# Gram products in three separate groups, their chain a period later, and layer 3's coefficients a quarter sooner

## The chip, the cores and the metric

The kernel runs on one core of a Trainium2 chip. The metric is the device time of one execution in microseconds (us), the median over several runs. One execution was also taken by the hardware profiler; all busy times, waits and timelines below come from it.

## What is computed

The input x has 16 images of 64 channels with 128 by 128 points, float32. Four layers follow, each of the form x = x + f(gn(x)), where gn is a group normalization over pairs of channels.

```
x = x + conv_w · (gram(gn(x)) · gn(x))      # layer 0: gram = gn(x) gn(x)^T / N, per image
x = x + |kx * gn(x)| + |ky * gn(x)|         # layer 1: two fixed 3x3 filters
x = x + conv3x3(shift(gn(x)), W) + b        # layer 2: some channels shifted by one column
x = x + clip(leaky(batchnorm(conv1x1(conv3x3(gn(x), w_bin)))), 0, 255)   # layer 3
```

Layer 0 needs the 64 by 64 matrix of channel products (the Gram matrix) of a whole image before the first point of that image can be made. From it the kernel works out one 64 by 64 mixing matrix for each image, with the normalization folded in, and the coefficients of layer 1's normalization. Layer 3's batch normalization is over all images, so the output is made in a last pass.

## The kernel before

An image is cut into 8 row blocks (`NS`), and the main loop runs over steps of four quarters, q0 to q3. In step s each stage works on the block `s - start - 8 b` of image b: `Front` (layers 0 and 1) starts at 15, `Layer2` at 25, `Layer3` at 35. So a period of 8 steps is one image for every stage, and three images are in work at once. Each engine gets its instructions in the order in which the loops write them down (`InOrder`), and nothing is reordered afterwards: an instruction that waits holds everything behind it on its engine.

In a step TensorE makes layer 3's products in q0 and q1 (first into `one`, with weights `w`, then into `two`), the mixing products `po` in q1, and layer 2's in q2 and q3 (`one` and `two`, with weights `wi`). There is one buffer `one` only. ScalarE (ACT) copies it out with the bias: `c<-one,b_sb` at the start of q1 for layer 3, and `c<-one,co` at the start of q3 for layer 2. The next product into `one` can't start before that copy is done. ACT also normalizes (`v`, `xh`), takes absolute values (`u`, `e`), squares for the statistics (`junk`), copies layer 3's half of the differences (`qd<-d`), and takes the square roots of the coefficient chains (`sd<-nv`). VectorE (DVE) makes layer 1's filter sums (`u`, `e`), the differences `d`, adds `x` and `y`, and does nearly all of the small arithmetic. GpSimd (POOL) scales edge columns and starts the DMAs of layer 2's copies `qd<-d`. SyncE (SP) starts the loads and stores.

The Gram products of the images from 7 on (class `Gram`) are made far ahead of their use. In eight steps the image's rows are loaded in 8 pieces of 512 KB (`xr`, three buffers) and copied by ACT into `xw`, one piece at a time (`rows_to_columns`). Then come 128 products of 65 columns in three parts of 44, 42 and 42 (`part`), which add up in one region of the PSUM bank `bank`. The same bank holds the results of all small products. Then `gram_chain` starts: a generator that alternates small products on TensorE with small arithmetic on DVE, a piece for each call of `tick()`, which comes at the end of each quarter. From the copy `gs` to the last `co` it runs through 17 quarters.

`coefficients` is a shorter chain of four quarters: a reduction of the sums, a product, a square root, and the coefficients. Layer 3's starts in q1 of the step in which layer 2 has finished the image (`i == NS`), after the last block's squares. `Layer3.prepare(0)` uses them one step later in q1; there DVE also makes `edge_lower` and `edge_upper` first.

For the period that is looked at below, steps 84 to 91: the Gram parts are those of image 12 (q0 and q2 of step 85, q0 of step 86); the chain of image 12 runs from q2 of step 86 to q2 of step 90; the copies into `xw` are those of image 13; layer 3's coefficients are those of image 7 (q1 of step 89 to q0 of step 90).

Of the kernel before, what the change touches and what calls it, by code (L numbers as in the profile page):

```python
# [10 lines left out]
F32 = mybir.dt.float32  # L11
# [97 lines left out]
def tile_kernel(ctx: ExitStack, tc: tile.TileContext, x, cw_h, w2_t, b2, wbin_t, w1_t, b1, gamma, beta, consts, out):  # L109
# [141 lines left out]
                    )  # L251


    chains = []

    def tick():
# [45 lines left out]

    def gram_chain(b, pg):

        gs = stp.tile([P, C + 1], F32, tag="gs", name=f"gs_{b}", bufs=1)
        dve.tensor_copy(gs, pg)
        if b > 1:
            yield
        gd = sm(C + 1)
        small_product(gd, k("same"), gs)  # L310
        yield
        g = stp.tile([P, C + 1], F32, tag="g", name=f"g_{b}", bufs=1)
        dve.tensor_scalar_mul(g, gd, 1.0 / HW)
        mu = g[:, C:C + 1]
        st = sv("st0", 2)
        dve.tensor_copy(st[:, 0:1], mu)

        junk0 = stp.tile([P, C], F32, tag="junk0", name=f"junk0_{b}", bufs=1)
        dve.scalar_tensor_tensor(
            junk0, g[:, 0:C], GN_EPS, k("Id"), op0=ALU.add, op1=ALU.mult, accum_out=st[:, 1:2]  # L320
        )
        if b > 1:
            yield
        pm = sm(2)
        small_product(pm, k("gavg"), st)
        yield
        r, me = sv("r"), sv("me", 2)
        yield from rstd(pm, r, me)

        vv = sv("vv", 3)  # L330
        dve.tensor_copy(vv[:, 0:1], mu)
        dve.tensor_sub(vv[:, 1:2], mu, me[:, 0:1])
        dve.tensor_scalar_mul(vv[:, 2:3], me[:, 0:1], -1.0)
        dd = stp.tile([P, 2, C], F32, tag="dd", name=f"dd_{b}", bufs=1)
        for s in range(2):
            dve.tensor_scalar_mul(dd[:, s, :], k("Id"), vv[:, s:s + 1])
        if b > 1:
            yield

        pr = sm(2 * C)  # L340
        small_product(pr, k("all"), dd.rearrange("p s c -> p (s c)"))
        yield

        t0 = stp.tile([P, C], F32, tag="t0", name=f"t0_{b}", bufs=1)
        dve.scalar_tensor_tensor(t0, pr[:, 0:C], vv[:, 0:1], g[:, 0:C], op0=ALU.mult, op1=ALU.subtract)
        cs = stp.tile([P, 2, C], F32, tag="cs", name=f"cs_{b}", bufs=1)
        for s in range(2):
            dve.scalar_tensor_tensor(cs[:, s, :], pr[:, C:2 * C], vv[:, 1:2], t0, op0=ALU.mult, op1=ALU.subtract)
        rc = stp.tile([P, C], F32, tag="rc", name=f"rc_{b}", bufs=1)
        dve.tensor_scalar(rc, cwh, r, 0.5, op0=ALU.mult, op1=ALU.mult)  # L350
        csf = cs.rearrange("p s c -> p (s c)")
        if b > 1:
            yield
        pq = sm(C)
        small_product(pq, csf, rc)
        yield
        r2 = sv("r2")
        dve.tensor_mul(r2, r, r)
        for s in range(2):
            rows = slice(s * C, (s + 1) * C)  # L360
            dve.tensor_scalar_mul(wbd[rows, rows], pq[rows], r2[rows])
        ad = stp.tile([P, C], F32, tag="ad", name=f"ad_{b}", bufs=1)
        dve.scalar_tensor_tensor(ad, pq, r2, k("Id"), op0=ALU.mult, op1=ALU.add)
        abd = stp.tile([P, P], F32, tag="abd", name=f"abd_{b}", bufs=EARLY + 3)
        dve.tensor_add(abd, wbd, k("I"))
        if b > 1:
            yield
        pd = sm(C + 3)
        small_product(pd[:, 0:C], csf, ad)
        small_product(pd[:, C:C + 2], abd, vv[:, 0:2])  # L370
        small_product(pd[:, C + 2:C + 3], wbd, vv[:, 2:3])
        yield
        pp = stp.tile([P, 2, C], F32, tag="pp", name=f"pp_{b}", bufs=1)
        dve.tensor_mul(
            pp, pd[:, 0:C].unsqueeze(1).to_broadcast([P, 2, C]), ad.unsqueeze(1).to_broadcast([P, 2, C])
        )
        av = sv("av", 3)
        dve.tensor_copy(av, pd[:, C:C + 3])
        if b > 1:
            yield  # L380
        pk = sm(1)
        small_product(pk, pp.rearrange("p s c -> p (s c)"), k("q"))
        if b > 1:
            yield
        bias = av[:, 2:3]
        st1 = sv("st1", 2)
        dve.tensor_add(st1[:, 0:1], av[:, 0:1], bias)
        t = sv("t1")
        dve.scalar_tensor_tensor(t, av[:, 1:2], av[:, 1:2], pk, op0=ALU.mult, op1=ALU.subtract)
        dve.scalar_tensor_tensor(  # L390
            st1[:, 1:2], st1[:, 0:1], st1[:, 0:1], t, op0=ALU.mult, op1=ALU.subtract
        )
        if b > 1:
            yield
        pm = sm(2)
        small_product(pm, k("gavg"), st1)
        yield

        co = stp.tile([P, 5], F32, tag="co1", name=f"co1_{b}", bufs=EARLY + 3)
        r, mean = co[:, 0:1], co[:, 3:4]  # L400
        yield from rstd(pm, r, co[:, 3:5], GN_EPS)
        dve.scalar_tensor_tensor(co[:, 1:2], bias, mean, r, op0=ALU.subtract, op1=ALU.mult)
        dve.reciprocal(co[:, 2:3], r)
        lead[b] = abd, co

    def gram_product(pg, w):

        s = w % 2
        pe.matmul(
            pg[s * C:(s + 1) * C, :], xw[:, w // 2, 0:C, s], xw[:, w // 2, :, s],  # L410
            start=(w < 2), stop=(w >= W - 2),
        )
        last[0] = s

# [8 lines left out]
    def first_gram():  # L423
# [13 lines left out]
        for m in range(NS + 1):  # L437
# [5 lines left out]
                    copy(xw[:, m * R:(m + 1) * R, 0:C, h], two[:, :, h * C:(h + 1) * C])  # L443
            if m > 0:
                for w in range(2 * R * (m - 1), 2 * R * m):
                    gram_product(pg, w)
        run(Front, 0, Front.first, 0)
        live[Front, 0].load(1)

# [6 lines left out]
                rows_to_columns(1, link - 2, rows[link - 2])  # L456

    class Gram:
        first, last = 0, NS + 1

        def __init__(self, b):
            self.b, self.xr, self.w = b, {}, 0

        def at(self, i, q):
            b = self.b
            if i < NS:
                if q == 0 and i != 1:
                    for m in range(i + (1 if i == 2 else 2) if i else 0, min(i + 3, NS)):
                        self.load(m)

                if q == 3 and i > 0:
                    for m in (0, 1) if i == 1 else (i,):
                        rows_to_columns(b, m, self.xr.pop(m))
                return
            n = 4 * (i - NS) + q

            self.part({0: 44, 2: 42, 4: 42}.get(n, 0))
            if n == 6:
                chains.append(gram_chain(b, self.pg))

        def part(self, n):
            if self.w == 0 and n:
                if self.b <= 2 * EARLY:
                    self.pg = ps_g.tile([P, CP, W], F32, tag="g", name=f"pg_{self.b}")[:, 0, 0:C + 1]
                else:

                    self.pg = bank[:, 3 * P:3 * P + C + 1]
            for _ in range(n // 2):
                for s in (1 - last[0], last[0]):
                    gram_product(self.pg, self.w + s)  # L490
                self.w += 2

        def load(self, m):
# [242 lines left out]
    class Layer2:  # L736
# [42 lines left out]
        def twin(self, n):  # L779
# [5 lines left out]
                flat(q[cols(1 - i), n])[:, 1:CP * (W + 2)], flat(d[cols(i), n])[:, 0:CP * (W + 2) - 1]  # L785
            )

        def square(self, i):
            act.activation(
                junk, tiles3[self.b][i].rearrange("p s j w -> p (s j w)"), AF.Square,  # L790
# [3 lines left out]
        def at(self, i, q):  # L794
            b = self.b
            closing = i + 1 == NS
            m = CP - 1 if closing else CP
            if q == 0:
                if 1 <= i:
                    two = self.p.pop(i - 1)[0]  # L800

# [13 lines left out]
            if q == 1:  # L815
# [25 lines left out]
                    pool.tensor_scalar_mul(t[:, :, W - 1], t[:, :, W - 1], k("keep1"))  # L841
                if i + 2 < NS:
                    self.load(i + 2)
                if i == NS:
                    self.square(i - 1)
                    chains.append(coefficients(self.st, lambda co: coefs3.update({b: co})))
            if q == 2:
                if 0 <= i < NS:
                    t = self.v[i]
# [26 lines left out]
            if q == "first of 3" and 0 <= i < NS:  # L876
                self.c = ring.tile([P, CP * W], F32, tag="c2", name=f"c2_{b}_{i}", bufs=1)
                act.activation(self.c, flat(self.p[i][1]), AF.Identity, bias=self.co[:, 5:6])
            if q == "last of 3" and -1 <= i < NS - 1:
                difference("d2", 1, self.v[i + 1], CP if i + 2 < NS else CP - 1)  # L880
                self.twin(1)
# [2 lines left out]
    class Layer3:  # L884
# [5 lines left out]
        def prepare(self, i):  # L890
# [5 lines left out]
                act.activation(dst, src, AF.Identity, bias=co[:, 1:2], scale=co[:, 0:1])  # L896

            if i == 0:
                self.co = coefs3.pop(b)

                self.edge = {}
                for half in ("lower", "upper"):
                    self.edge[half] = sv(f"edge_{half}", 2)
                    dve.tensor_scalar_mul(self.edge[half], self.co, k(half))
                norm(t[:, 0, :], tiles[NS - 1][:, 1, CP - 1, :], self.edge["lower"])
            else:
                norm(t[:, 0, :], tiles[i - 1][:, 1, CP - 1, :], self.co)
# [112 lines left out]
            fetched[0] += 1  # L1020

    for step in range(starts[2][1] - 2, steps):
        for q in range(4):
            for b in range(B):

# [5 lines left out]
            for stage, at in starts:  # L1031
                if stage is Front and q in (1, 3):
                    issue_rest()
                for b in range(B):
                    run(stage, b, step - at - NS * b, q)
            if q == 3:
                for b in range(B):
                    run(Layer2, b, step - starts[1][1] - NS * b, "last of 3")
            for b in range(1, B):
                at, n = pace[b]  # L1040
                if n == 1:
# [113 lines left out]
```

## Time and profile before

| | us |
|---|---|
| median of 3 runs | 2779.61 (2778.61 to 2780.83) |
| the profiled execution | 2778.27 |
| its span, first to last instruction | 2776.5 |
| TensorE busy | 2175.3 (78%) |
| DVE busy | 2192.0 (79%) |
| ACT busy | 2112.6 (76%) |
| POOL busy | 893.2 (32%) |

The span lacks 1.8 us that lie around the instructions. The shares are averages over a start of some 300 us, the main loop to about 2120 us, layer 3's last steps on TensorE to about 2320 us, and the last pass, which moves data only. In the lines of the profile each group is named by what it writes and reads, as in `two<-d,w`. The helper that keeps the order makes nearly every instruction carry the same source line, so the names and the engine tell them apart. A product in float32 leaves two records.

### The profile page before, as it was taken

Reading aid. Unit: us, or ns where it says so; the run is one execution under the profiler, and the core shown is the slowest. Engines: PE = TensorE matmul, PEld = TensorE weight load, DVE = VectorE, ACT = ScalarE, POOL = GpSimd, SP = SyncE. Lnnn points to the kernel's source line nnn. Section 1 sums busy time; section 2 is a strip of 40 time slices with the busy share of each in tenths; the row PEclk is TensorE's granted clock in tenths of the full one; section 3 lists DMA queues with packets and bytes.
Section 4 is the critical chain, followed back from the end, with each engine's and each line's share of the span. In section 5 each row is a group of like instructions: output and inputs, shape, how many; then the busy total and the mean of one; then the engine's idle time right before and its main releaser. Section 6 shows DMA issues by size and latency. Waiting matters only on the chain. (4 is left out here: it accounts for less than half of the span.)

```text
span 2776.5 us, 46105 instructions
## 1 busy us (share of the span) xinstructions
PE 2175.3 (78%) x14804; PEld 886.4 (32%) x14804; DVE 2192.0 (79%) x3623; ACT 2112.6 (76%) x3177; POOL 893.2 (32%) x1350
## 2 busy tenths in 40 slices
PE   6578899999999999999999999999999994000000
PEld 4233433434343434343433342333334641000000
DVE  4999999898989898989899999999996435333332
ACT  4766889898989898989898988999997667333332
POOL 2055434343434343434343344444444300000000
PEclk8689999999999999999999999999999997555555
DMA  8799888988888888888888777878877768999999
GB/s 205 201 229 238 211 216 226 231 215 229 218 227 213 229 221 221 216 230 216 230 218 227 206 188 197 217 202 219 215 199 195 213 196 288 420 420 420 420 420 384
DMA packets 693601, 685.96 MB, mean 247 GB/s; under 512 B 60096, under 2 KB 580448, under 8 KB 693360
## 3 DMA queue, kind: packets, MB, share of 16 engines
q1 hardware_dynamic: 668208, 613.83, 75.2%
q0 software_dynamic: 25152, 69.18, 10.2%
q8 instruction: 119, 1.95, 0.3%
q14 instruction: 122, 1.00, 0.1%
HBM read 346.23 MB, written 268.44 MB: 221 GB/s over the span
## 5 line engine op out<-in xcount | busy, mean ns | idle before, releaser
L73 PE MATMUL two<-d,w 128*64 128x508 f32 (+2 forms) x2560 | 846.8, 588 | 0.0
L73 PE MATMUL two<-d,wi 128*64 128x508 f32 (+3 forms) x1536 | 578.0, 579 | 0.0
L73 POOL DMA_DIRECT2D qd<-d x512 | 270.8, 531 | 903.7 <-DVE d L73 287.4
L73 PE MATMUL two<-qd,pk 128*64 128x512 f32 (+1 forms) x1024 | 519.0, 588 | 13.3 <-DMA qd<-d 12.5
L73 POOL TENSOR_SCALAR edges<-v,co 64x8 f32<-64x8 f32 x512 | 359.9, 703 | 307.7 <-ACT v L73 231.4
L73 DVE TENSOR_TENSOR d<-v 128x512 f32<-128x512 f32 (+1 forms) x512 | 345.6, 678 | 87.6 <-issue 55.5
L73 PE MATMUL one<-v,w 128*64 128x508 f32 (+2 forms) x1600 | 378.6, 599 | 34.8 <-ACT c L73 34.8
L73 PEld LDWEIGHTS two<-d,w 128*64 128x64 f32 x2560 | 263.1, 136 | 314.9 <-issue 278.5
L73 PE MATMUL one<-v,wi 128*64 128x508 f32 (+3 forms) x1536 | 358.5, 599 | 3.1 <-issue 2.6
L73 ACT COPY qd<-d 64x512 f32<-64x512 f32 x512 | 315.4, 616 | 20.8 <-DVE d L73 14.5
L73 DVE SCALAR_TENSOR_TENSOR e<-e 128x1032 f32<-128x1032 f32 (+1 forms) x256 | 312.9, 1222 | 0.0
L73 ACT ACTIVATE xh<-po,co 128x128 f32<-128x128 f32 (+1 forms) x480 | 275.2, 621 | 31.4 <-PE po L73 22.7
L73 POOL TENSOR_SCALAR v<-v,kc 128x9 f32<-128x9 f32 x256 | 234.6, 930 | 12.0
L73 DVE SCALAR_TENSOR_TENSOR y<-two,c 128x1024 f32<-128x1024 f32 x128 | 155.9, 1218 | 102.8 <-ACT v L73 65.4
L73 PEld LDWEIGHTS two<-d,wi 128*64 128x64 f32 x1536 | 175.6, 136 | 186.0 <-issue 169.6
L73 ACT ACTIVATE v<-x,co 128x512 f32<-128x512 f32 (+2 forms) x368 | 234.9, 705 | 0.0
L73 ACT ACTIVATE u<-u 128x1024 f32<-128x1024 f32 x128 | 135.3, 1057 | 106.8 <-DVE u L73 106.4
L73 PE MATMUL po<-x,abd 64*64 64x512 f32 (+1 forms) x1024 | 178.5, 643 | 44.0 <-ACT xh L73 41.0
L73 PEld LDWEIGHTS one<-v,w 128*64 128x64 f32 x1600 | 126.0, 139 | 237.9 <-issue 162.7
L73 PEld LDWEIGHTS two<-qd,pk 128*64 128x64 f32 x1024 | 136.3, 136 | 153.9 <-issue 110.6
L73 PEld LDWEIGHTS one<-v,wi 128*64 128x64 f32 x1536 | 108.9, 138 | 224.1 <-issue 209.0
L73 DVE SCALAR_TENSOR_TENSOR u<-xh 128x1170 f32<-128x1170 f32 x128 | 175.6, 1371 | 5.1 <-ACT xh L73 4.2
(165 smaller groups left out, 3333.9 us busy)
## 6 DMA issues: line engine op xcount, KB each, us to landing
x<-in_x SPq DMA_DIRECT2D x256, 256.0 KB, 4.1
x_d<-u SPq DMA_DIRECT2D x512, 128.0 KB, 3.8
y_d<-y SPq DMA_DIRECT2D x512, 128.0 KB, 4.0
x_d<-x SPq DMA_DIRECT2D x496, 128.0 KB, 2.6
xr<-in_x SPq DMA_DIRECT2D x120, 512.0 KB, 6.4
qd<-d POOLq DMA_DIRECT2D x256, 130.0 KB, 3.1
qd<-d POOLq DMA_DIRECT2D x256, 129.8 KB, 3.9
v<-x_d SPq DMA_DIRECT2D x448, 72.1 KB, 3.3
```

The costliest lines, as they stand in the source:

```text
L73: return self.tc.keep_in_program_order(call(*args, **kwargs))
```

## The change

Four things are changed, for the images from 7 on in the first three.

- The three parts of the Gram products stand in q1 of three successive steps (85, 86 and 87 in the period above) and are three groups, each started and closed by itself in a region of its own (`first`, `end`, `at`). `gram_chain` begins with a reduction over the three regions in place of a copy.
- The chain makes that reduction in q2 of step 87, and then waits until step `8 b - 4` before it goes on. So the chain of image 11 runs from q0 of step 84 to q3 of step 87, between the Gram parts of image 12. The buffer `gs` is doubled.
- Loads and copies of the row pieces are laid out anew: copies in q3 of step 87, q1 and q3 of 88, q3 of 89, q1 and q3 of 90, q3 of 91 and of 92; three loads in q0 of step 87, and each later one right behind a copy.
- For all images, layer 3's coefficient chain begins one quarter earlier, in q0, with the last block's squares at the end of that quarter, and the two `edge` vectors are made at its end instead of in `prepare`.

```
+    now = [0]
...
     def gram_chain(b, pg):
-        gs = stp.tile([P, C + 1], F32, tag="gs", name=f"gs_{b}", bufs=1)
-        dve.tensor_copy(gs, pg)
+        gs = stp.tile([P, C + 1], F32, tag="gs", name=f"gs_{b}", bufs=2)
+        if b > 2 * EARLY:
+            dve.tensor_reduce(gs, pg.rearrange("p (j c) -> p c j", j=3), axis=AX.X, op=ALU.add)
+        else:
+            dve.tensor_copy(gs, pg)
         if b > 1:
             yield
+        while b > 2 * EARLY and now[0] < NS * b - 4:
+            yield
...
-    def gram_product(pg, w):
+    def gram_product(pg, w, first, end):
...
-            start=(w < 2), stop=(w >= W - 2),
+            start=(w < first + 2), stop=(w >= end - 2),
...
     class Gram:
-        first, last = 0, NS + 1
+        first, last = 2, NS + 2
...
-            if i < NS:
-                if q == 0 and i != 1:
-                    for m in range(i + (1 if i == 2 else 2) if i else 0, min(i + 3, NS)):
-                        self.load(m)
-                if q == 3 and i > 0:
-                    for m in (0, 1) if i == 1 else (i,):
-                        rows_to_columns(b, m, self.xr.pop(m))
-                return
-            n = 4 * (i - NS) + q
-            self.part({0: 44, 2: 42, 4: 42}.get(n, 0))
-            if n == 6:
-                chains.append(gram_chain(b, self.pg))
+            n = 4 * (i - NS) + q
+            self.part({1: 44, 5: 42, 9: 42}.get(n, 0))
+            if n == 10:
+                chains.append(gram_chain(b, self.pg))
+            if i == 2 and q == 0:
+                for m in range(3):
+                    self.load(m)
+            m = {11: 0, 13: 1, 15: 2, 19: 3, 21: 4, 23: 5, 27: 6, 31: 7}.get(4 * i + q)
+            if m is not None:
+                rows_to_columns(b, m, self.xr.pop(m))
+                if m + 3 < NS:
+                    self.load(m + 3)
...
-                    self.pg = bank[:, 3 * P:3 * P + C + 1]
+                self.pg = bank[:, 2 * P:2 * P + 3 * (C + 1)]
+                first, end, at = self.w, self.w + n, self.parts * (C + 1)
+                self.parts += 1
             for _ in range(n // 2):
                 for s in (1 - last[0], last[0]):
-                    gram_product(self.pg, self.w + s)
+                    gram_product(self.pg[:, at:at + C + 1], self.w + s, first, end)
...
     class Layer2:
+        def done(self, co):
+            edge = {}
+            for half in ("lower", "upper"):
+                edge[half] = sv(f"edge_{half}", 2)
+                dve.tensor_scalar_mul(edge[half], co, k(half))
+            coefs3[self.b] = co, edge
...
             if q == 0:
+                if i == NS:
+                    chains.append(coefficients(self.st, self.done))
...
-                if i == NS:
-                    self.square(i - 1)
-                    chains.append(coefficients(self.st, lambda co: coefs3.update({b: co})))
...
+            if q == "last of 0" and i == NS:
+                self.square(i - 1)
...
     class Layer3:
             if i == 0:
-                self.co = coefs3.pop(b)
-                self.edge = {}
-                for half in ("lower", "upper"):
-                    self.edge[half] = sv(f"edge_{half}", 2)
-                    dve.tensor_scalar_mul(self.edge[half], self.co, k(half))
+                self.co, self.edge = coefs3.pop(b)
...
     for step in range(starts[2][1] - 2, steps):
+        now[0] = step
...
-            if q == 3:
+            if q in (0, 3):
                 for b in range(B):
-                    run(Layer2, b, step - starts[1][1] - NS * b, "last of 3")
+                    run(Layer2, b, step - starts[1][1] - NS * b, f"last of {q}")
```

More of the change, by code (lines that the diff above doesn't have):

```diff
@@ L445, in first_gram @@
                 for w in range(2 * R * (m - 1), 2 * R * m):
-                    gram_product(pg, w)
+                    gram_product(pg, w, 0, W)
         run(Front, 0, Front.first, 0)
@@ L458, in tile_kernel, with part @@
     class Gram:
-        first, last = 0, NS + 1
+        first, last = 2, NS + 2
         def __init__(self, b):
-            self.b, self.xr, self.w = b, {}, 0
+            self.b, self.xr, self.w, self.parts = b, {}, 0, 0
         def at(self, i, q):
             b = self.b
-            if i < NS:
-                if q == 0 and i != 1:
-                    for m in range(i + (1 if i == 2 else 2) if i else 0, min(i + 3, NS)):
-                        self.load(m)
-                if q == 3 and i > 0:
-                    for m in (0, 1) if i == 1 else (i,):
-                        rows_to_columns(b, m, self.xr.pop(m))
-                return
-            n = 4 * (i - NS) + q
-            self.part({0: 44, 2: 42, 4: 42}.get(n, 0))
-            if n == 6:
-                chains.append(gram_chain(b, self.pg))
-        def part(self, n):
-            if self.w == 0 and n:
-                if self.b <= 2 * EARLY:
+            n = 4 * (i - NS) + q
[10 more added lines that the diff above has]
+                    self.load(m + 3)
+        def part(self, n):
+            if not n:
+                return
+            first, end, at = 0, W, 0
+            if self.b <= 2 * EARLY:
+                if self.w == 0:
                     self.pg = ps_g.tile([P, CP, W], F32, tag="g", name=f"pg_{self.b}")[:, 0, 0:C + 1]
-                else:
-                    self.pg = bank[:, 3 * P:3 * P + C + 1]
+            else:
+                self.pg = bank[:, 2 * P:2 * P + 3 * (C + 1)]
+                first, end, at = self.w, self.w + n, self.parts * (C + 1)
+                self.parts += 1
             for _ in range(n // 2):
                 for s in (1 - last[0], last[0]):
-                    gram_product(self.pg, self.w + s)
+                    gram_product(self.pg[:, at:at + C + 1], self.w + s, first, end)
                 self.w += 2
```

## The prediction

> **What bounds the kernel now.** I read the slices of the page first, then the busy time of each engine in the windows of one period of eight steps, then the timelines around the one place where TensorE is idle.
>
> ```profile
> PE   6578899999999999999999999999999994000000
> DVE  4999999898989898989899999999996435333332
> ACT  4766889898989898989898988999997667333332
> ```
>
> From slice 5 to slice 32 all three engines are near full. An average can't say which one sets the pace, so I cut out the period in which image 12's Gram products are made, steps 84 to 91; each window goes from one start of layer 3's copy `c<-one,b_sb` (q1) to the next. Columns: stretch, length, busy time of PE, PEld, DVE, ACT, POOL, granted clock, DMA.
>
> ```profile
> 1158.00:1172.60 14.60, 14.60 (x90) 5.03 (x88) 14.23 (x20) 14.50 (x24) 7.17 (x10) 1.00 0.79 207
> 1172.60:1191.00 18.40, 18.40 (x230) 9.32 (x227) 13.76 (x18) 14.86 (x27) 5.00 (x10) 1.00 0.94 235
> 1191.00:1210.10 19.10, 19.10 (x170) 7.91 (x168) 16.15 (x29) 16.40 (x24) 5.42 (x10) 1.00 0.75 190
> 1210.10:1226.10 16.00, 16.00 (x90) 5.31 (x88) 15.55 (x40) 15.38 (x27) 5.94 (x10) 1.00 1.06 257
> 1226.10:1242.90 16.80, 16.80 (x134) 9.34 (x132) 16.40 (x29) 15.06 (x25) 6.06 (x10) 1.00 0.91 244
> 1242.90:1260.50 17.60, 16.80 (x95) 5.51 (x91) 17.29 (x31) 15.57 (x27) 8.06 (x10) 1.00 0.84 231
> 1260.50:1279.70 19.20, 15.04 (x66) 4.51 (x66) 18.55 (x39) 15.29 (x27) 5.98 (x11) 0.91 0.81 222
> 1279.70:1294.60 14.90, 14.90 (x74) 4.68 (x72) 14.53 (x20) 14.80 (x24) 7.41 (x11) 1.00 0.75 182
> ```
>
> TensorE is busy for the whole of six windows: it is the bound, and only the windows of steps 89 and 90 leave it idle, 0.80 + 4.16 us. There DVE is the fullest. DVE has time to spare in steps 85 and 86, where all three Gram parts stand (18.4 - 13.8 and 19.1 - 16.2 us), and none from 87 to 90, where the chain's vector work stands. The same period without Gram work (steps 116 to 123) takes 122.7 us, TensorE busy 122.0. Now the idle place, TensorE first, then ACT:
>
> ```profile
> 1265.80 1.03 PE L73 MATMUL two<-d,wi 128*64 128x508 f32 x4
> 1268.42 0.61 PE L73 MATMUL two<-qd,pk 128*64 128x512 f32 x1 [1.59 <-DMA qd<-d]
> ...
> 1272.92 4.48 PE L73 MATMUL one<-v,w 128*64 128x512 f32 x12 [2.57 <-ACT c L73]
> ```
>
> ```profile
> 1260.50 0.69 ACT L73 ACTIVATE c<-one,b_sb 128x512 f32<-128x512 f32 x1
> 1262.94 0.49 ACT L73 ACTIVATE v<-x,edge_lower 128x128 f32<-128x128 f32 x1 [1.75 <-DVE edge_lower L73]
> ...
> 1268.14 0.20 ACT L73 ACTIVATE sd<-nv 128x1 f32<-128x1 f32 x1 [2.05 <-DVE nv L73]
> ```
>
> TensorE waits 2.57 us for ACT to copy `one` out. ACT is late because it sat 1.75 us waiting for layer 3's coefficients and 2.05 us for the chain's last square root. After this idle time the twelve products take 4.48 us where they take 2.73 us elsewhere (at 1289.5): the clock is at half. So a period with Gram work loses 0.80 + 4.16 + (4.48 - 2.73) = **6.7 us**. Both late inputs are what the change moves.
>
> [...] 4.48 against 2.73 us after 1.59 + 2.57 us of idle time; a wait of 0.70 us in step 89 has no such tail. [...] In the changed order each Gram part waits for a DVE read of `bank`: part 2 for `ad`, made in q0 of its own step.
>
> **Part by part, for one period.** *Gram parts.* 256 product records before and after; the 88 of one part take 2.94 us, of the others 2.78. Moving them is worth nothing in itself: TensorE's total stays. But part 3 goes from step 86 to 87, which holds TensorE back 2.8 us just ahead of the steps where DVE and ACT are short.
>
> *Chain.* Its vector work is 0.47 + 0.36 + 1.2 + 0.86 + 1.28 + 0.27 + 0.45 + 0.71 + 1.04 = 6.6 us on DVE (from `g` at 1209.5 to `co` at 1272.2, less what stands between). It leaves 87 to 90 and goes to 84 to 87, where its last 2.2 us stay. Steps 84 to 86 take some 4.5 us more, within the 7.6 us spare in 85 and 86. Up to q0 of step 90 DVE is freed of 2.7 us. The reduction of three parts in place of a copy: 0.22 us for 65 elements, about 1 ns more an element (`pp`, 128 elements, 0.28): estimate 0.35 us, so +0.13, in step 87 behind TensorE. Waits added on TensorE for DVE: in 85 and 86 DVE's inputs lie 4 to 14 us ahead of the products, so none; in 87, where `gs` must wait for part 3, DVE arrives about when it ends: 0 to 1 us of DVE time, taken 0.
>
> *Copies into `xw`* (1.18 us on ACT): before two in step 86, one each in 87 to 92; now none in 86, two in 88 and in 90. Queued behind those is `c<-one,co`, for which TensorE waits.
>
> *Coefficients of layer 3.* The edge wait (1.75) and the chain's root (2.05) leave step 90. New in step 89: `junk<-x` before `c<-one,b_sb` (1.15 us that ACT did a little later before), DVE's reduction behind it, and the root in q2. Freed DVE is some 4.9 us earlier at `x` in step 89, but must then stand still for about 2 us until ACT has squared it; `nv` is ready about 1.7 us after ACT gets to the root.
>
> *SP and POOL.* No POOL instruction moves. Three row loads of 512 KB go from step 85 to 87, the others right behind their copies; SP holds stores of `y`, `x` and `u` behind them, none waited for soon. One load issued at 1260.46 stood before the twin of 1262.29 that landed after 6.0 us (median 3.8). I take 0; the bound is 1.6 us a period in either direction.
>
> *What is late next.* ACT. Between two copies `c<-one,co` it has 15.4 us of work in a step with one `xw` copy and 16.6 with two; TensorE takes 14.85 from one layer-3 `one` to the next in a step without other work (1289.51 to 1304.36), about 15.6 to 16 in step 88 (closing rows). ACT's lead can be at most 3.6 us: after layer 2's `one` is done TensorE has 4.3 us left before the next `one`, less 0.7 for the copy. It was 1.5 us at step 88 (copy done 1219.3, product 1220.9); with part 3 ahead of it I put it at 3.6. Then: step 88, 16.6 against 16.0, lead 3.0. Step 89, 16.0 + 0.5 + 1.7 of waits against 14.7: lead used up, TensorE waits 0.7. Step 90, 16.6 against 14.9: 1.7. Step 91, 15.4 against 14.85: 0.6. New waits 3.0 us[...]. Gain 6.7 - 3.0 = **3.7 us** for each of nine images (7 to 15): 33 us. The last chain falls into steps 116 to 119, with DVE 58.5 us busy of 59.9: its 5 us cost perhaps 2 there, about what its own period gains more for want of `xw` copies. In the periods without a moved chain only the coefficients count: TensorE waits 0.7 us for the copy at 1805 and 2.2 us plus half clock at 1927: 5 us together. Sum 38 us against the profiled execution's 2778.3 us: 2740; the median shown is 1.3 us above it, so **2742 us**.
>
> **Rivals.** *A, all of it comes back:* the ACT waits don't build up, because the granted clock or the copies fall luckier: 9 x 6.7 + 8 = 68 us, 2712. For it: TensorE's full windows. Against: ACT's 16.6 us. *B, slower by ACT:* ACT becomes the bound of steps 88 to 91, because it doesn't get its lead of 3.6 us in step 87 (waiting for `nv`, which waits for part 3). With a lead of 1.5 the waits are 2.8 + 1.7 + 0.6 = 5.1 us, and two of these in a row bring half clock, 1.75 each: 8.6 against 6.7 us, +17 us, less 5 for the rest: 2792. It decides from new waits of 7.2 us a period on. For it: ACT is full in steps 91 and 92 (14.80 of 14.90 us). Against: in 85 to 87 ACT waits for TensorE. *C, the wait only moves:* new waits equal to the old, 2775 to 2785. That the change doesn't do what it says is excluded: in the changed order the chain's products stand between the Gram parts, and `sd` of layer 3 ahead of `c<-one,co`.
>
> **Numbers.** My forecast 0.58, A 0.16, C 0.08, B 0.18. About 0.2% (5.6 us) is what a measurement of this kernel can tell from no change. Faster 0.77 (forecast, A and part of C), same 0.06, slower 0.17. The forecast's own range is 2724 to 2762 (1.6 us a period both ways, the last chain 0 to 4); with A and the near half of B it is 2716 to 2788.
>
> **What would show it.** Right: periods of 132 to 134 us where they were 136.6; step 90 short (15 to 17 us), no ACT wait for `edge_lower`; an ACT wait for `nv` of 1 to 2 us in step 89; TensorE waiting for `c` under 2 us a step. Wrong: half clock again in step 91, or TensorE waiting for DVE in steps 84 to 87.

## The result, and the profile after

The changed kernel takes **2756.91 us** (median of 4 runs, 2756.63 to 2757.97); the kernel before, in the same session, took 2779.11 us (4 runs). The ratio is 0.992, with a 95% interval of 0.990 to 0.994: about 22 us faster. 2742 us was predicted, with a range of 2716 to 2788, so the side was right and the size was 15 us too large. The profiled execution took 2756.86 us, its span 2755.1 us, against 2776.5 us before.

The slices of the page look the same as before. They can't show a difference of 0.8%:

```profile
PE   6578799999999999999999999999999994000000
DVE  4998899899999999999999999999996335333332
ACT  4766779998989898989898989899997667333332
```

The windows of steps 84 to 91 can. Cut as before, from one start of `c<-one,b_sb` to the next (columns: stretch, length, busy time of PE, PEld, DVE, ACT, POOL, granted clock, DMA share, GB/s):

```profile
1146.70:1161.50 14.80, 14.80 (x78) 4.78 (x76) 14.59 (x25) 14.70 (x25) 4.40 (x10) 1.00 0.81 217
1161.50:1177.70 16.20, 16.20 (x166) 7.51 (x164) 15.91 (x31) 14.84 (x27) 7.40 (x10) 1.00 0.81 202
1177.70:1194.10 16.40, 16.40 (x168) 7.40 (x166) 15.63 (x27) 14.13 (x24) 7.71 (x10) 1.00 0.71 184
1194.10:1212.30 18.20, 18.20 (x168) 7.68 (x166) 16.43 (x43) 15.54 (x25) 7.48 (x10) 1.00 1.00 247
1212.30:1231.20 18.90, 18.90 (x130) 10.26 (x126) 17.03 (x25) 17.37 (x28) 9.46 (x12) 1.00 0.93 260
1231.20:1248.20 17.00, 15.31 (x78) 4.70 (x76) 16.47 (x30) 14.58 (x26) 6.04 (x9) 1.00 0.87 224
1248.20:1264.20 16.00, 15.02 (x74) 4.59 (x72) 15.85 (x23) 15.91 (x25) 7.28 (x12) 1.00 0.93 254
1264.20:1279.20 15.00, 15.00 (x78) 4.73 (x76) 14.64 (x20) 14.91 (x25) 7.16 (x12) 1.00 0.85 228
```

The period is 132.5 us long where it was 136.6. The Gram parts now stand in steps 85, 86 and 87, whose windows hold 166, 168 and 168 records of TensorE; it has no idle time there, and DVE has become full (15.91 of 16.20 us in step 85). Step 90, 19.2 us before, takes 16.0, and the clock is whole in every window. TensorE is idle in steps 89 and 90 only, 1.69 and 0.98 us, in front of layer 3's `one`. The timeline of TensorE around these two places:

```profile
1241.49 2.78 PE L73 MATMUL one<-v,w 128*64 128x512 f32 x12 [1.69 <-ACT c L73]
...
1257.54 2.78 PE L73 MATMUL one<-v,w 128*64 128x512 f32 x12 [0.98 <-ACT c L73]
```

Neither is followed by products at half clock: twelve take 2.78 us. The timeline of ACT says why the copy is late in step 89. The root of layer 3's coefficients, moved ahead of the copy, waits for DVE:

```profile
1240.66 0.20 ACT L73 ACTIVATE sd<-nv 128x1 f32<-128x1 f32 x1 [1.41 <-DVE nv L73]
1240.77 0.67 ACT L73 ACTIVATE c<-one,co 128x512 f32<-128x512 f32 x1
```

DVE is late with `nv` because it stood still for 1.73 us in q0 of this step: the reduction of the sums waits for ACT's squares (`junk`), which the change has moved ahead of it. From here to `nv` DVE has no gap. The timeline of DVE:

```profile
1231.35 0.17 DVE L73 TENSOR_REDUCE s<-st 128x2 f32<-128x16 f32 x1 [1.73 <-ACT junk L73]
```

ACT in turn works without a gap from the root to the copy of `one` at 1256.80 in step 90, so its lateness carries over to that step.

**Where the time went** over the whole kernel, from the same copy's starts in both profiled executions (us, to the first copy of step 44, then by stretches of steps):

| | to 44 | 44-107 | 108-115 | 116-123 | 124 to the end | span |
|---|---|---|---|---|---|---|
| before | 477.7 | 1090.1 | 135.3 | 122.7 | 950.7 | 2776.5 |
| after | 486.0 | 1058.1 | 129.7 | 128.9 | 952.3 | 2755.1 |
| difference | +8.4 | -32.1 | -5.6 | +6.2 | +1.7 | -21.4 |

So the nine periods with moved Gram work gain 37.6 us, more than the 33 predicted, and 16 us are given back elsewhere: at the start, in the period of the last chain, and 1.7 us after it. (The last is hardly more than chance: three kernels below without early coefficients or a slowed chain differ from the kernel before by 0.2 to 1.4 us there.) Most of the start's loss is at one place. The timeline of TensorE in step 33, after the change:

```profile
298.57 0.38 PE L73 MATMUL bank<-s,kc 128*64 128x2 f32 x4 [7.34 <-DVE g L73]
298.81 5.34 PE L73 MATMUL one<-v,wi 128*64 128x512 f32 x12
```

and before the change, where layer 3's product `bank<-s,kc` comes later:

```profile
292.05 2.79 PE L73 MATMUL one<-v,wi 128*64 128x512 f32 x12 [1.30 <-issue]
```

The small product for layer 3's coefficients waits 7.34 us, until DVE has made `g`, which belongs to the Gram chain of another image. DVE's reading of `bank` for `g` stands ahead of the product in program order, behind some 6 us of DVE's queue. The product writes other columns (`sm` in the kernel gives two-column results the first 128 columns and wider ones those behind), but the same bank, and it waits for that read; all of TensorE waits behind it. Its own input was there earlier. The timeline of DVE after the change:

```profile
292.59 0.17 DVE L73 TENSOR_REDUCE s<-st 128x2 f32<-128x16 f32 x1 [0.67 <-ACT junk L73]
...
298.30 0.22 DVE L73 TENSOR_SCALAR g<-bank 128x65 f32<-128x65 f32 x1
```

So the first 1.5 us of the wait are for `s`, the other 5.8 us for the bank. Then twelve products run at half clock: they take 5.34 us, and the granted clock is 0.50 over them, where it was 1.00 over the 2.79 us before.

### The profile page after: what moved, and what is told of

It is laid out like the page before. It is cut to its first block, busy times and chain, and to the rows that moved or that the text cites. A ratio compares the mean times of both kernels' runs of the same rounds, so it can differ in the third digit from the quotient of the medians.

```text
span 2755.1 us, 46091 instructions
## 1 busy us (share of the span) xinstructions
PE 2159.6 (78%) x14804; PEld 886.9 (32%) x14804; DVE 2192.4 (80%) x3623; ACT 2113.5 (77%) x3177; POOL 943.2 (34%) x1350
## 5 line engine op out<-in xcount | busy, mean ns | idle before, releaser
L73 PE MATMUL two<-d,w 128*64 128x508 f32 (+2 forms) x2560 | 837.5, 587 | 0.0
L73 POOL TENSOR_SCALAR edges<-v,co 64x8 f32<-64x8 f32 x512 | 397.7, 777 | 287.4 <-ACT v L73 204.0
L73 PE MATMUL one<-v,w 128*64 128x508 f32 (+2 forms) x1600 | 364.6, 580 | 30.1 <-ACT c L73 30.1
L73 POOL TENSOR_SCALAR v<-v,kc 128x9 f32<-128x9 f32 x256 | 246.7, 976 | 11.9
```

Of the source, the lines that this page charges most:

```text
L73: return self.tc.keep_in_program_order(call(*args, **kwargs))
```

## Experiments

All ratios are to the kernel before, run in the same batch (medians of 2778.8 to 2779.7 us). First the overview: the profiled span, and its difference to the kernel before by stretches of steps (us). Kernels that are alike up to step 44 still differ in the first column by up to 4 us (e8_no_hold and e12_last_quarter_pace).

| kernel | median | to 44 | 44-107 | 108-115 | 116-123 | 124 to the end |
|---|---|---|---|---|---|---|
| after | 2756.9 | +8.4 | -32.1 | -5.6 | +6.2 | +1.7 |
| e1_gram_only | 2738.2 | +0.9 | -42.5 | -5.8 | +5.9 | +0.2 |
| e2_coef_only | 2820.0 | +9.9 | +28.5 | +3.3 | 0.0 | +1.6 |
| e11_coef_first | 2782.8 | +3.9 | +0.7 | -0.8 | 0.0 | +1.1 |
| e3_coef_not_0 | 2750.4 | +0.5 | -30.4 | -5.6 | +6.2 | +1.1 |
| e4_last_free | 2759.5 | +7.2 | -32.3 | +4.3 | +0.1 | +1.1 |
| e6_copies | 2763.4 | +8.7 | -25.3 | -4.6 | +6.2 | +1.5 |
| e7_part3_86 | 2756.4 | +7.8 | -32.2 | -5.6 | +6.2 | +1.6 |
| e8_no_hold | 2764.4 | +2.8 | -13.3 | -1.1 | -0.2 | +0.2 |
| e9_last_free | 2738.0 | -0.2 | -42.3 | +0.2 | -0.2 | +1.4 |
| e13_last_half_pace | 2738.1 | +0.4 | -42.5 | -5.8 | +5.1 | +1.0 |
| e12_last_quarter_pace | 2738.8 | -1.4 | -42.2 | -5.8 | +2.6 | +3.3 |

### The two halves of the change

**The Gram part alone** (e1_gram_only). The changed kernel, with layer 3's coefficients where they were before:

```
             if q == 0:
-                if i == NS:
+                if i == NS and not (b >= 0):
                     chains.append(coefficients(self.st, self.done))
...
                 if i + 2 < NS:
                     self.load(i + 2)
+                if i == NS and b >= 0:
+                    self.square(i - 1)
+                    chains.append(coefficients(self.st, self.done))
...
-            if q == "last of 0" and i == NS:
+            if q == "last of 0" and i == NS and not (b >= 0):
```

> The changed kernel with layer 3's coefficients started where they were before (q1, squares in q1, for all images); Gram parts, chain and row copies stay as changed. My theory: the moved chain alone frees DVE so far that the old coefficient chain no longer makes ACT wait at step 90, while the early one costs a standstill of DVE for the last block's squares and a late square root in step 89. So the period of eight steps falls from 132.5 to about 130.5 us, and the start, which became 5.9 us longer, goes back to what it was: about 2735 us. Rival (the early coefficients are what removed the waits of step 90): the wait for edge_lower, 1.75 us, comes back in each period, periods of about 134 us, 2760 us or a little less with the start repaired.

Measured: 2738.24 us, ratio 0.985 (0.984 to 0.987). That is near the theory's 2735. **The early coefficients are a loss of 19 us in the changed kernel**, and about 10 of these lie in the Gram periods, where they were meant to help: a period takes 131.2 us instead of 132.5. The timelines of TensorE and ACT of this kernel:

```profile
1242.30 2.78 PE L73 MATMUL one<-v,w 128*64 128x512 f32 x12 [1.39 <-ACT c L73]
```

```profile
1233.50 0.49 ACT L73 ACTIVATE v<-x,edge_lower 128x128 f32<-128x128 f32 x1 [1.52 <-DVE edge_lower L73]
```

ACT's wait for `edge_lower`, 1.75 us before the change, is still there with 1.52 us, and it costs TensorE one wait of 1.39 us. The early coefficients take that wait away, but their own standstill of DVE and the late `nv` cost TensorE 1.69 + 0.98 us. The difference, 1.28 us, is that of the periods.

**The coefficients alone** (e2_coef_only). The kernel before with only the last part of the change (`done`, the `edge` vectors and the call of "last of 0" as above):

```
             if q == 0:
+                if i == NS:
+                    chains.append(coefficients(self.st, self.done))
...
-                if i == NS:
-                    self.square(i - 1)
-                    chains.append(coefficients(self.st, lambda co: coefs3.update({b: co})))
...
+            if q == "last of 0" and i == NS:
+                self.square(i - 1)
```

> The kernel before with only the coefficients of layer 3 a quarter sooner (for all images). My theory: in the periods with Gram work DVE is still full, so ACT waits longer for nv in step 89 than it saves at edge_lower in step 90: periods of 136 to 138 us against 136.6; the start is longer by 6 us, because the product of image 0's coefficients now stands in the same quarter as a vector piece of image 5's chain and is held until DVE has read the shared bank. About 2785 us, 2780 to 2797. Rival (the two halves of the change add up, the coefficients bring about half): periods of 134.5 us and no longer start, 2760 us.

Measured: 2820.04 us, ratio 1.014 (1.013 to 1.016). Neither expectation allowed for a loss of 41 us: the first had foreseen the wait at the bank for the start only. The waits of TensorE, summed over the whole span (what waited, for whom: us in total, times, longest), have the answer in one line:

```profile
PE bank L73 <- DVE av L73: 56.7, 11, 6.3
```

In the kernel before that line reads

```profile
PE bank L73 <- DVE av L73: 6.5, 11, 0.8
```

It is the start's wait again. Here the chain of the image isn't moved and runs through step 89, so in every period layer 3's product stands behind a read of `bank` by the chain, and TensorE stands with it. In step 89 (timeline of TensorE):

```profile
1279.13 0.38 PE L73 MATMUL bank<-s,kc 128*64 128x2 f32 x4 [6.15 <-DVE av L73]
```

The timeline of DVE shows that here nearly the whole wait is for the bank: the product's input `s` is ready 6 us before, and the product starts right behind the chain's read.

```profile
1273.02 0.17 DVE L73 TENSOR_REDUCE s<-st 128x2 f32<-128x16 f32 x1 [0.67 <-ACT junk L73]
...
1278.92 0.15 DVE L73 COPY av<-bank 128x3 f32<-128x3 f32 x1
```

**The coefficients alone, written ahead of the chain's piece** (e11_coef_first). To show that the order at the bank is the cause, and not the earlier work itself, one thing is changed in the last kernel: in q0 and q1 layer 3's coefficients are first in the list of chains, so that their reduction and their product stand ahead of the Gram chain's pieces, and the product ahead of the chain's read.

```
-                    chains.append(coefficients(self.st, self.done))
+                    self.chain = coefficients(self.st, self.done)
+                    chains.insert(0, self.chain)
...
+            if q == 2 and i == NS:
+                chains.remove(self.chain)
+                chains.append(self.chain)
```

> Coefficients of layer 3 a quarter sooner on the kernel before, but in q1 their product is written down ahead of the Gram chain's vector piece, and from q2 on behind it. So the product waits for its own reduction only, and no longer for that vector piece's reading of the shared bank. My theory (the wait of 6 us per image in step 89 is the wait for the bank in program order): TensorE's wait before bank<-s goes to under 1 us, step 89 from 20.9 to about 18, periods of 134 to 136.5 us, first layer-3 copy near 326 us, 2765 to 2782 us. Rival (the standstill of DVE for the squares and the late root cost the time, not the bank): periods stay near 139.7 us, 2815 us.

Measured: 2782.83 us (20 runs), ratio 1.0012 (1.0005 to 1.0018). This is just above what the theory gave (2765 to 2782) and far from the rival. The order at the bank was worth 37 us. The early coefficients without that wait change the periods by less than 1 us in all. A loss of 3 us remains; the profiled execution has it at the start (+3.9 us), where like kernels differ as much. The same line of TensorE's waits:

```profile
PE bank L73 <- DVE av L73: 7.1, 11, 0.8
```

**Only the first image's coefficients late** (e3_coef_not_0). In the changed kernel, image 0 gets its coefficients as before, all others a quarter early:

```
-                if i == NS:
+                if i == NS and not (b == 0):
                     chains.append(coefficients(self.st, self.done))
...
+                if i == NS and b == 0:
+                    self.square(i - 1)
+                    chains.append(coefficients(self.st, self.done))
...
-            if q == "last of 0" and i == NS:
+            if q == "last of 0" and i == NS and not (b == 0):
```

> The changed kernel, image 0's coefficients of layer 3 alone started as before. My theory: TensorE's wait of 7.3 us at 291 us and the half clock after it are gone, the first layer-3 copy comes at about 325.5 instead of 331.4 us, all else stays: 2751 us. Rival (the longer start comes from the first row loads or from another part of the change): 2757 us, start at 331 us.

Measured: 2750.42 us, ratio 0.989 (0.988 to 0.991), and the first copy `c<-one,b_sb` starts at 325.5 us, as before (325.4), instead of 331.4. (Among the kernels made from the changed one this start lies at 330.3 to 331.9 us in the four with image 0's coefficients early, and at 323.8 to 328.4 in the five with none early.) So the loss at the start comes from image 0's early coefficients, and with them the 7.34 us wait of their product is gone from TensorE's waits.

### The parts of the Gram half

**The hold** (e8_no_hold). The kernel with the Gram part alone, without the hold; the chain of image 12 then runs from q2 of step 87 to step 91:

```
-        while b > 2 * EARLY and now[0] < NS * b - 4:
-            yield
```

> The changed kernel with the old coefficients of layer 3 (as in the kernel of 2738 us), and the chain not held until the next image's Gram steps: it runs from q2 of step 87 to step 91. My theory (the gain comes from moving the chain's vector work out of 88 to 90): the waits in steps 89 and 90 return, with half clock, periods of 135 to 137 us, 2770 to 2790 us. Rival (the three spread parts are what brings it): 2738 to 2745 us.

Measured: 2764.44 us, ratio 0.995 (0.993 to 0.996); between the two. Of the 41 us of the Gram part the hold brings 26, the new places of parts, loads and copies the other 15. Without the hold TensorE waits 2.07 us for the chain and 0.92 + 1.42 us for `c`, 4.4 us together against 1.39 with it, and the clock stays whole in these steps (granted 1.00), against the theory.

**The place of part 3** (e7_part3_86). The changed kernel with part 3 in q3 of step 86 instead of q1 of step 87:

```
-            self.part({1: 44, 5: 42, 9: 42}.get(n, 0))
+            self.part({1: 44, 5: 42, 7: 42}.get(n, 0))
```

> The changed kernel with the third part of the Gram products in q3 of step 86 in place of q1 of 87. My theory (part 3 in step 87 gives ACT and DVE the lead with which they enter step 88): TensorE's waits in steps 89 and 90 grow by about 2 us together, periods of 134.5 us, 2773 us. Rival (TensorE's total is the same, so the place of the part is worth nothing): 2757 us.

Measured: 2756.44 us, ratio 0.992 (0.990 to 0.993), the same as the changed kernel; the waits in steps 89 and 90 are 1.75 and 0.97 us. So the rival holds: ACT's lead, the time by which its copy of `one` is done ahead of TensorE's next product, doesn't come from this place, where the prediction had sought it.

**The copies into `xw`** (e6_copies). One each in steps 88 to 91 in place of two in 88 and two in 90; the last three move to q1 and q3 of step 92 and q0 of step 93:

```
-            m = {11: 0, 13: 1, 15: 2, 19: 3, 21: 4, 23: 5, 27: 6, 31: 7}.get(4 * i + q)
+            m = {11: 0, 15: 1, 19: 2, 23: 3, 27: 4, 29: 5, 31: 6, 32: 7}.get(4 * i + q)
```

> The changed kernel with the copies into xw laid out one a step: q3 of 87 to 90, then q1 and q3 of 92, q0 of 93 and q3 of 91 (none in q1 of 88 and of 90). My theory (ACT with two copies in steps 88 and 90 is what is late next, and holds up DVE through the squares): the waits of 1.69 and 0.98 us for the copy of one in steps 89 and 90 fall to about 0.7 and 0, periods of about 130.5 us, 2740 us; if ACT then has too little lead in 92 and 93, part of it comes back there. Rival (the late root, a DVE matter, sets both waits): no change, 2757 us.

Measured: 2763.43 us, ratio 0.995 (0.993 to 0.996): slower than the changed kernel by 6.5 us, against both expectations. The three copies of steps 92 and 93 fall into one window between two copies `c<-one,b_sb`, and there ACT has work for the whole of it, and DVE nearly. The same window one image earlier, of step 84, is 14.8 us long in the changed kernel and 16.8 in this one:

```profile
1151.10:1167.90 16.80, 16.80 (x90) 5.30 (x90) 16.48 (x35) 16.70 (x27) 5.67 (x12) 1.00 0.86 235
```

TensorE's waits for `c` add up to more, and in more places: 37.0 us in 36 waits, where the changed kernel has 30.1 us in 27.

So the layout moved the crowd and didn't spread it, and its total time doesn't decide between the two expectations. But its steps 88 to 91, with one copy each, answer the question: they take 66.7 us where the changed kernel takes 66.9, with waits of 1.78 and 0.78 us in steps 89 and 90 where that has 1.69 and 0.98. The second copies are not what makes ACT late there.

### The last chain

The chain of image 15 falls into steps 116 to 119, where no Gram products stand. It costs 6.2 us there, where 2 were predicted.

**Not held,** in the changed kernel (e4_last_free):

```
-        while b > 2 * EARLY and now[0] < NS * b - 4:
+        while 2 * EARLY < b < B - 1 and now[0] < NS * b - 4:
```

> The changed kernel, but the chain of the last image (15) doesn't wait for step 116: it runs from the end of step 111 on, as there is no later image whose Gram steps it could use. My theory: steps 116 to 123 fall from 128.9 us back to about 122.6, and steps 108 to 115 grow from 129.7 by 2 to 4 us, since the chain's vector work is then in the steps where DVE is short: 2753 to 2755 us. Rival (the last chain costs its 6 us wherever it stands): 108 to 115 grow by 6 us and the time is 2757 us.

Measured: 2759.45 us, ratio 0.993 (0.991 to 0.995). Steps 116 to 123 are back at 122.8 us, but 108 to 115 take 139.6 instead of 129.7: the free chain meets the early coefficients of image 10 at the bank. That is above both expectations. TensorE's waits in steps 112 and 113 of this kernel:

```profile
PE bank L73 <- DVE cs L73: 5.8, 1, 5.8
```

**Not held, or slower, without the early coefficients.** Three kernels from the one with the Gram part alone. The first (e9_last_free) has the edit just shown:

> The kernel with the Gram part of the change alone (coefficients of layer 3 as before the change; 2738.2 us), but the chain of the last image, 15, is not held: it runs from step 111 on instead of in steps 116 to 119. Theory: in steps 116 to 119 the held chain costs 6.2 us (128.6 us for the period that takes 122.4 without it), because DVE is full there (17.2 of 17.5 us in step 117) and no Gram products give it time. Free, it costs 4 to 6 us in the period from step 108 instead (129.5 to about 134.5), where no copies into xw stand; steps 116 to 123 come back to 122.5. Sum 2736 to 2738. Rival: what made the kernel with the early coefficients slower there (9.9 us) was the chain itself and not the meeting with the coefficients at the bank; then 139 us for the period from 108, and 2741 to 2743.

The other two (e13_last_half_pace, e12_last_quarter_pace) spread the last chain, one piece in every second or fourth quarter (`k` is 2 or 4; `quarter` is set beside `now`):

```
+    def slow(c):
+        for _ in c:
+            yield
+            while now[0] >= NS * (B - 1) - 4 and (now[0], quarter[0]) < due[0]:
+                yield
+            if now[0] >= NS * (B - 1) - 4:
+                n = 4 * now[0] + quarter[0] + k
+                due[0] = n // 4, n % 4
...
-                chains.append(gram_chain(b, self.pg))
+                c = gram_chain(b, self.pg)
+                chains.append(slow(c) if b == B - 1 else c)
```

> The kernel with the Gram part of the change alone (2738.2 us), but the chain of the last image takes one piece in every second quarter: it runs through steps 116 to 124. Theory (DVE is full in 116 to 119 and has some 4 us free in 120 to 123): between the full pace and the quarter pace, the period from 116 at 124.5 to 127, sum 2735 to 2737. Rival (the chain costs the same wherever it stands): 2737 to 2739.

> The kernel with the Gram part of the change alone (2738.2 us), but the chain of the last image takes one piece in every fourth quarter: it runs through steps 116 to 132 instead of 116 to 119. Its instructions are the same. Theory: the chain costs 6.2 us in steps 116 to 119 because DVE is full there; at a quarter of the pace its 6.6 us of DVE work falls into time that DVE has free (about 1 us in a step without a chain), so the period from 116 comes down from 128.6 to 123 to 125, the one from 124 rises from 122.4 by at most 2, and the sum is 2733 to 2736. Rival: the chain costs its small products on TensorE and their waits wherever it stands; then what the first period loses the second gains, and it stays at 2737 to 2739.

Measured: 2738.01, 2738.11 and 2738.79 us, ratios 0.985, 0.985 and 0.986 (each 0.984 to 0.987). None differs from the kernel that holds the chain (2738.24). Taking the three periods from 108, 116 and 124 together, against their length without the last chain (129.5 us and twice 122.4), the last chain costs 6.5 us where it is free (6.1 of them in the period from 108, which goes from 129.5 to 135.5), 6.1 at full pace, 6.2 at half pace and 6.2 at a quarter (125.3 + 125.8 us where two periods without it take 122.4 each). With the early coefficients the free chain lengthened the period from 108 by 9.9 us, so about 4 of these come from the meeting at the bank. The theory that DVE has time free that a slower chain could use falls; the rival, that the chain costs the same wherever it stands, is right for these steps. TensorE's waits in steps 116 to 123 rise from 0.7 us before the change to 5.3 after it, 4.1 of them for ACT's copies of `one`. The windows of steps 117 and 119 after the change show that DVE, with TensorE's 0.5 to 1.2 us of idle time beside it, is fullest there:

```profile
1688.60:1706.10 17.50, 16.99 (x92) 5.59 (x90) 17.21 (x33) 14.80 (x27) 8.46 (x10) 1.00 0.80 201
...
1722.10:1738.50 16.40, 15.21 (x82) 4.80 (x80) 15.91 (x42) 14.34 (x25) 7.40 (x10) 1.00 0.91 234
```

6.1 to 6.5 us is close to the chain's own vector work, 6.6 us as the prediction added it up. That fits steps that DVE paces, but no run changed that work by itself, so it is argued and not shown. In the Gram steps 84 to 87 TensorE paces, and there the chain is nearly free: in the kernel with the Gram part alone, the period from 108 holds the Gram parts of image 15 and the chain of image 14 and takes 129.5 us, no more than 122.4 us and the 8.5 us of the Gram products themselves (2.94 + 2.78 + 2.78).

## Why the prediction was right, and where it was wrong

- **The bound and the 6.7 us of a period: right.** What TensorE lost in steps 89 and 90 and to half clock was what there was to gain: with the Gram part alone the period gains 5.4 us and keeps a wait of 1.39, 6.8 together.
- **New waits, 0.7 + 1.7 + 0.6 = 3.0 us: right in sum, not in place.** Measured are 1.69 (step 89), 0.98 (step 90) and none (step 91), 2.7 us; the `nv` wait, put at about 1.7, is 1.41. The gain of a period is 4.2 us (37.6 / 9) where 3.7 were predicted. All signs that the prediction named as right came (periods of 132.5 us, step 90 of 16.0, no wait for `edge_lower`, a wait for `nv`, waits for `c` under 2 us), though a half of the change was a loss: they couldn't tell the halves apart. The sum counted no half clock behind these waits, and in all nine periods none came (granted clock 1.00 from 486 to 1676 us), with little room: e9_last_free has half clock after a single wait of 1.94 us (last section).
- **The working behind these waits: wrong.** The prediction had ACT's lead rise from 1.5 to 3.6 us because part 3 goes to step 87. The lead did rise, to 3.4 us ahead of step 88's product, but with part 3 in step 86 it is 3.1 us and the time is the same (e7_part3_86). Without the hold it is 3.5 us (e8_no_hold), so the chain's new place doesn't raise it either; the other new places of parts, loads and copies are left, and which of them does it was not isolated. With one copy in steps 88 and 90 the waits should nearly have gone; they stayed (e6_copies). So ACT's second copies don't set them, and that 3.0 us came out in sum is luck in part. In the trace DVE's standstill and the late `nv` stand ahead of them. The prediction had this standstill (about 2 us, measured 1.73) in its sum; it didn't see that it would cost more than the wait for `edge_lower`, which alone costs 1.39 us.
- **The coefficients: the wrong sign, and the largest error.** The prediction gave the early coefficients the whole merit of the vanished `edge` wait and 5 us in the periods without a chain. The runs show a loss of 10 us in the Gram periods and about 7 at the start; 1.5 more late in the kernel are within what like kernels differ by. Without them the change takes 2738.2 us. That this lies near the predicted 2742 is luck, since the prediction counted gains by the coefficients in its sum.
- **The start, counted at nothing: a term that was missing.** The prediction had looked at the shared bank for the Gram parts only, and found the chain moved out of layer 3's way. For the images whose chain isn't moved, the move of a product by one quarter puts it behind a foreign read. Every product that changes place has to be checked against the reads of its bank in program order, in every stage of the kernel; the prediction left that step out. Rival B, a loss by ACT, didn't occur; the mechanism that can turn such an edit into a loss is this one, 41 us in the kernel before (e2_coef_only).
- **The last chain, put at 2 us: measured 6.2.** Its own period, from 108, gains 5.6 us, so the last image loses 0.6. The prediction took DVE's 1.4 us of spare time in four steps as room; the runs show that hardly anything of the chain fits beside the other work there, at any of three paces.

Rival A (2712) left out that any of this is given back; even the kernel without the early coefficients keeps 1.4 us of waits a period. Rival C's waits equal to the old ones didn't come.

The half clock of TensorE the runs show behind a long wait (5.34 against 2.79 us behind 7.34 us of idle time), and 1.69 us brought none; but it also came after single waits of 1.94 and 2.07 us, and one wait of 2.66 us brought it where an equal one didn't (last section). That each Gram part has to be a group of its own was not shown, since it is one in each kernel with interleaved parts. And the shared bank carried the case, not by the Gram parts, which waited for nothing (TensorE has no idle time in steps 85 to 87), but by a product of 0.4 us, which waited 7.34 and 6.15 us, most of it for reads of other columns of its bank.

**The best version** of those tried is the Gram part without the early coefficients: 2738.24 us, 0.985 of before and 0.993 of the changed kernel (2738.24 / 2756.91). Where the last chain stands makes no difference to it.

## What to carry to other kernels

When a small instruction is moved to an earlier place, look up which reads and writes of the same buffer now stand ahead of it in program order, in every stage and for every image, and what those wait for; a product of 0.4 us held TensorE for 6 to 7 us. Serial side work belongs in the steps that another engine paces: here the chain was nearly free beside the Gram products, and cost 6.1 to 6.5 us in the steps without them, at each of three paces. Run each half of a combined change alone before crediting both, since here one half gave 41 us and the other took 19 back.

## What was not expected of the hardware

In these runs the length of a wait of TensorE doesn't decide alone whether its clock falls. In e11_coef_first the same wait, one period later at the same place of the program, brought half clock once and left the clock whole once; it is the only wait of TensorE in the 7 us before. The timeline of TensorE:

```profile
867.33 4.33 PE L73 MATMUL one<-v,w 128*64 128x512 f32 x12 [2.66 <-ACT c L73]
...
1004.42 2.78 PE L73 MATMUL one<-v,w 128*64 128x512 f32 x12 [2.66 <-ACT c L73]
```

Single waits of 1.94 us (e9_last_free, at 2007.92: 4.48 us for twelve products) and of 2.07 us (before, at 1927.64: 4.10, the granted clock down to 0.50) brought half clock, and one of 2.98 us (e12_last_quarter_pace, at 1758.47: 2.78) did not. Of pairs, 2.07 and 0.92 us with 2.9 us of work between them left it whole in e8_no_hold, and 1.59 and 2.57 us with 1.9 us of work between them brought half clock in the kernel before. So what a wait of 2 to 3 us cost here can't be told from its length. What else decides it no run tested. Beyond that the runs showed nothing new of the chip; the surprises were in the order of the program.
